# The last pair of a two-layer graph network: elu, residual sums and stores by quarters

## The chip, the cores and the metric

The kernel runs on one core of one Trainium2 chip. The metric is the device time of one execution in microseconds (us). A run's time is a little longer than the span of the profile, which goes from the first to the last instruction on the core.

## The reference, cut to what matters

The input x has 128 batches of 128 rows with 512 features, and adj is one 128 by 128 matrix a batch. Layer 0 is multi-head attention with eight heads, layer 1 a graph attention layer; both normalise their input first, and both are added to x. The change touches the end of layer 1, which is `h_prime`, `elu` and the last sum.

```python
# layer 0
h = maximum(layernorm(x), 0)
x = x + attention(h, adj, Wq, bq, Wk, bk, Wv, bv, Wo, bo)
# layer 1
h = maximum(layernorm(x), 0)
Wh = h @ W
e = leaky_relu(Wh @ a[:512] + transpose(Wh @ a[512:]), 0.2)
att = softmax(where(adj > 0.5, e, -9e15), axis=1)
h_prime = att @ Wh
x = x + elu(h_prime)          # elu(z) = z for z > 0, exp(z) - 1 otherwise
```

## The kernel before

The work goes by pairs of batches: p runs over 64 pairs. A pair's rows are held in `xs[p]`, a tile of 128 partitions (the rows of a batch) by 2 batches by 512 features in fp32. All of it is unrolled: each pair has a table of named steps (`steps`, L636 to L707), and three lists written out by hand say in which order the steps are issued, `HEAD` for the start, `ORDER` for the steady part, where steps of several pairs are interleaved, and `TAIL` for the last pairs (L569 to L606). In `TAIL`, `w4@-1` is step w4 of the last pair and `fb@-2` is step fb of the last but one. Each engine (PE for matmuls, ACT, DVE, POOL) and the SP queue, which issues the DMAs, takes its own instructions in this order; engines wait for each other with semaphores.

Layer 1 is computed as att @ h first and then times W. The product with W is done by a scheme with seven block products instead of eight (`PRODUCTS`, L124): the pair's two batches are the two row blocks t, and two halves of the features are the column blocks f. So the result z of a pair (a tile of 128 by 2 by 512) falls into four quarters (t, f) of 128 by 256, which `quarter(t, f)` selects. The steps w0, w1, w3, w2, w4, w5, w6 (`product_rows`, L282 to L292) are the seven products on TensorE, in that order. The steps zc0, zc2, zc4 and zc5 (`put1`, L463 to L467, on ACT) copy the first part of the quarters (0,0), (1,0), (1,1) and (0,1) out of PSUM, and wd1, wd4c and wd6 (`add1`, L469 to L471, on DVE) add a second part to the quarters (0,0), (1,1) and (1,0). So a quarter is complete at wd1 for (0,0), at wd4c for (1,1), at zc5 for (0,1) and at wd6 for (1,0), the last, which needs w6.

Then come four steps for the whole pair, with 1024 elements a partition each:

- ez (`elu`, L473 to L476): ez = exp(z), on ACT;
- fa (`finish_a`, L478 and L479): x = max(z, 0) + x, on DVE;
- fb (`finish_b`, L481 and L482): x = min(ez, 1) + x, on DVE. The -1 of elu is in a constant added earlier;
- so (`store`, L484 and L485): one DMA of 512 KB from the SP queue to `out`.

For every pair but the last these steps are interleaved with the work of later pairs. The list ends with the last pair's steps:

```
fb@-2 w2@-1 gs3@-1 zc2@-1 so@-2 w4@-1 zc4@-1 w5@-1 wd4c@-1 w6@-1 zc5@-1 wd6@-1 fa@-1 ez@-1 fb@-1 so@-1
```

Of the kernel before, what the change touches and what calls it, by code (L numbers as in the profile page):

```python
# [8 lines left out]
F32 = mybir.dt.float32  # L9
AF = mybir.ActivationFunctionType  # L10
OP = mybir.AluOpType
AX = mybir.AxisListType

P = 128
# [10 lines left out]
def kernel(  # L25
# [18 lines left out]
    nc = tc.nc  # L44
    B, S, E = x.shape
# [9 lines left out]
    work = ctx.enter_context(tc.tile_pool(name="work", bufs=1))  # L55
# [4 lines left out]
    xs, x0s, adjs, adjTs, hAs, hSs = {}, {}, {}, {}, {}, {}  # L60

    def both(src, p):
        return src[2 * p : 2 * p + 2].rearrange("b p f -> p b f")

    def load_x(p):

        xs[p] = io.tile([P, 2, E], F32, name="x")
        if p < 2:
            for i in range(2):
                nc.sync.dma_start(xs[p][:, i, :], x[2 * p + i])  # L70
        else:
            nc.sync.dma_start(xs[p], both(x, p))
# [96 lines left out]
    l1s, h1s, wts, pbs, pgs, gTs, zs, ezs, posts, hns, pts, onces = ({} for _ in range(12))  # L169
# [127 lines left out]
    def quarter(t, f):  # L297

        return slice(None), t, slice(f * 2 * P, (f + 1) * 2 * P)

    def scores(b):
        p, i = divmod(b, 2)
        g, h = divmod(p, 2)
        qT, kT = qks[g, "q"][h], qks[g, "k"][h]
        cols = slice(i * S, (i + 1) * S)

        sc = [ps1.tile([P, C, S], F32, name="sc", tag="ps1") for _ in range(2)]
        for j in range(C):
            for s in range(2):
                r = slice(s * D, (s + 1) * D)  # L310
                nc.tensor.matmul(sc[s][:, j, :], qT[r, j, cols], kT[r, j, cols], start=True, stop=True)  # L311
        scs[b] = sc
# [10 lines left out]
    def maxima(b):  # L323
        at, nmx, _, _ = ats[b]
        nc.vector.tensor_reduce(nmx, at, AX.X, OP.max, negate=True)  # L325
# [55 lines left out]
    def keep_context(b):  # L381
        nc.scalar.copy(rows_of(cxT, b % 2), pcs.pop(b))

    def output0(p, n):
        product_rows(p, cxT, wo_sb, "o", n)
# [84 lines left out]
        d = zs[p][quarter(t, f)]  # L470
        nc.vector.tensor_tensor(d, row_acc(p, "w", bank), d, OP.add)  # L471

    def elu(p):  # L473

        ezs[p] = work.tile([P, 2, E], F32, name="ez")
        nc.scalar.activation(ezs[p], zs[p], AF.Exp)  # L476

    def finish_a(p):  # L478
        nc.vector.scalar_tensor_tensor(xs[p], zs[p], 0.0, xs[p], op0=OP.max, op1=OP.add)  # L479

    def finish_b(p):  # L481
        nc.vector.scalar_tensor_tensor(xs[p], ezs.pop(p), 1.0, xs[p], op0=OP.min, op1=OP.add)  # L482

    def store(p):  # L484
        nc.sync.dma_start(both(out, p), xs.pop(p))  # L485
# [38 lines left out]
    N = B // 2  # L524
# [7 lines left out]
    def listed(text, mark):  # L532
# [69 lines left out]
        w5@-3 od6@-1 st1@-1 g0@-2 zc5@-3 st0@-1 g1@-2 ge0@-2 fa@-3 pw@-1 w0@-2 ge1@-2 ez@-3 gs2@-2 w1@-2 gs0@-2 gs1@-2  # L602
        w3@-2 nm@-1 zc0@-2 h20@-1 wd1@-2 w2@-2 h21@-1 d01@-1 d10@-1 zc2@-2 w4@-2 d00@-1 d11@-1 zc4@-2 pb@-1 wm@-1
        wd4c@-2 pr@-1 w6@-2 m1@-1 gs3@-2 e1@-1 w5@-2 sw@-1 fb@-3 zc5@-2 g0@-1 g1@-1 wd6@-2 ge0@-1 so@-3 fa@-2 w0@-1
        ge1@-1 ez@-2 gs2@-1 w1@-1 gs0@-1 gs1@-1 w3@-1 zc0@-1 wd1@-1 fb@-2 w2@-1 gs3@-1 zc2@-1 so@-2 w4@-1 zc4@-1 w5@-1
        wd4c@-1 w6@-1 zc5@-1 wd6@-1 fa@-1 ez@-1 fb@-1 so@-1  # L606
    """
    HEAD, ORDER, TAIL = listed(HEAD, "@"), listed(ORDER, ":"), listed(TAIL, "@")

    def start_steps(p):  # L610

        table = {}
        if 0 <= p < 4:
            table["pp"] = lambda: st0[p][2]()
            for i in range(2):
                table[f"hn{i}"] = lambda i=i: rows_hidden(p, i)
                table[f"tp{i}"] = lambda i=i: turn_hidden(p, i)
                table[f"ev{i}"] = lambda i=i: keep_hidden(p, i)
        if p == 0:
            weights = {"v": (wv_sb, wvT), "q": (wq_sb, wqT), "k": (wk_sb, wkT), "o": (wo_sb, woT), "w": (w1_sb, w1)}  # L620
            for n, (w, src) in weights.items():
                table["L" + n] = lambda w=w, src=src: nc.sync.dma_start(w[:, 0:4], src)
                for k in range(4):
                    table[f"W{n}{k}"] = lambda w=w, k=k: weight_sum(w, k)
            table |= {
                "Lc": lambda: load_row(c_sb, bo), "Lu0": lambda: load_row(us_sb, a1), "Lu1": lambda: load_row(ut_sb, a1, E),
                "ccp": product_c, "ccd": sum_c,
            }
            for i in range(2):
                table[f"sup{i}"] = lambda i=i: turn_u(i)  # L630
                table[f"sua{i}"] = lambda i=i: keep_u(i)
                for half in range(2):
                    table[f"cu{i}{half}"] = lambda i=i, half=half: dots_u(i, half)
        return table

    def steps(p):  # L636

        table = start_steps(p)
        for s, n in (("a", 2 * p), ("b", 2 * p + 1)):
            table |= {  # L640
                "sc" + s: lambda n=n: scores(n),
                "mx" + s: lambda n=n: maxima(n),
                "fl" + s: lambda n=n: flip_blocks(n),
                "bl" + s: lambda n=n: send_blocks(n),
                "pl" + s: lambda n=n: place_blocks(n),
                "pc" + s: lambda n=n: context(n),
                "pe" + s: lambda n=n: keep_context(n),
            }
            for k in range(4):
                table[f"ex{s}{k}"] = lambda n=n, k=k: exps(n, k)  # L650
                table[f"nm{s}{k}"] = lambda n=n, k=k: normalise(n, k)
            for k in range(2):
                table[f"at{s}{k}"] = lambda n=n, k=k: weigh(n, k)
                table[f"rc{s}{k}"] = lambda n=n, k=k: shares(n, k)
        for n in range(7):
            table[f"o{n}"] = lambda n=n: output0(p, n)
            table[f"w{n}"] = lambda n=n: output1(p, n)
        for k in range(4):
            table[f"cs{k}"] = lambda k=k: token_sum(cxT, cxT[:, 4:7], k)
            table[f"gs{k}"] = lambda k=k: token_sum(gTs[p], gTs[p][:, 4:7], k)  # L660
        for n, t, f in (("0", 0, 0), ("1", 0, 0), ("2", 1, 0), ("4", 1, 1), ("4c", 1, 1), ("5", 0, 1), ("6", 1, 0)):
            bank = "b" if n == "1" else "c" if n in ("4c", "6") else "a"
            table["od" + n] = lambda t=t, f=f, bank=bank: add0(p, t, f, bank)
            if bank == "a":
                table["zc" + n] = lambda t=t, f=f: put1(p, t, f)
            else:
                table["wd" + n] = lambda t=t, f=f, bank=bank: add1(p, t, f, bank)
        for i in range(2):
            table[f"st{i}"] = lambda i=i: stats1(p, i)
            table[f"h2{i}"] = lambda i=i: hidden1(p, i)  # L670
            table[f"g{i}"] = lambda i=i: gather1(p, i)
            table[f"ge{i}"] = lambda i=i: keep_gathered(p, i)
            for k in range(2):
                table[f"d{i}{k}"] = lambda i=i, k=k: dot1(p, i, k)
        table |= {
            "lt": lambda: load_adjT(p), "pw": lambda: l1s[p][2](), "nm": lambda: centre1(p), "pb": lambda: scores1(p), "wm": lambda: mask1(p),
            "pr": lambda: leaky1(p), "m1": lambda: maxima1(p), "e1": lambda: exps1(p), "sw": lambda: normalise1(p),
            "ez": lambda: elu(p), "fa": lambda: finish_a(p), "fb": lambda: finish_b(p), "so": lambda: store(p),
            "sh": lambda: shift(p),
        }  # L680
        table["lx"] = lambda: load_x(p)
        if p + 1 < N:
            table["la"] = lambda: load_adj(p + 1)
        if p + 4 < N:
            table |= {
                "f0": lambda: fetch0(p + 4), "lT": lambda: load_xT(p + 4),
                "hd0": lambda: hidden(p + 4, 0), "hd1": lambda: hidden(p + 4, 1),
            }
        if p + 5 < N:
            table |= {  # L690
                "l0": lambda: load_x0(p + 5), "t0": lambda: stats0(p + 5, 0), "t1": lambda: stats0(p + 5, 1),
                "s0": lambda: spread0(p + 5),
            }
        g, odd = divmod(p, 2)
        if odd and (g + 2) * 2 < N:
            for k in range(4):
                table[f"hs{k}"] = lambda k=k: hidden_sum(g + 2, k)
        if (g + 1) * 2 < N:
            for k, u in enumerate(SEQ[10:] if odd else SEQ[:10], 1):
                def unit(k=k, u=u):  # L700
                    posts[p, k] = product(g + 1, u[0], int(u[1]))
                table[f"U{k}"] = unit
                if int(u[1]) in FIRSTS:
                    table[f"F{k}"] = lambda k=k: posts[p, k][0]()
                if int(u[1]) in ADDS:
                    table[f"A{k}"] = lambda k=k: posts[p, k][1]()
        return table  # L707
# [59 lines left out]
```

## Time and profile before

| what | us |
|---|---|
| median of 4 runs | 2367.74 |
| lowest, highest | 2366.84, 2368.40 |
| the profiled execution's own time | 2368.2 |
| its span | 2366.4 |
| TensorE busy | 2340.9 |
| DVE busy | 2005.7 |
| ACT busy | 1437.9 |
| copy of one quarter, z<-row_a 128x256 (L467, ACT, mean) | 0.370 |
| add of one quarter, z<-row_c 128x256 (L471, DVE, mean) | 0.420 |
| exp of a pair, ez<-z 128x1024 (L476, ACT, mean) | 1.058 |
| x<-z,x 128x1024 (L479, DVE, mean) | 1.196 |
| x<-ez,x 128x1024 (L482, DVE, mean) | 1.218 |
| store out<-x of 512 KB (L485), issue to landing, smallest and median | 2.8, 6.0 |

Times of instructions are those of one profiled execution. They are given in microseconds from the start of the span. A busy time is the sum of what an engine's instructions took. In a group's line, the part behind "idle before" is the time in which the engine had nothing to run ahead of these instructions, and the name behind the arrow is what ended it. The DMA share is the mean busy share of the core's 16 DMA engines. The clock that TensorE was granted is 0.999 of full speed in this execution.

### The profile page before, as it was taken

How to read it: one execution, taken by the hardware profiler on the slowest of the kernel's cores; microseconds unless marked ns; L12 is line 12 of the kernel's file. 1: busy time of each engine (PE TensorE's matmuls, PEld its weight loads, DVE VectorE, ACT ScalarE, POOL GpSimd, SP SyncE). 2: the span in 40 equal slices, each digit the busy share in tenths (PEclk: the TensorE clock that was granted, in tenths of full speed). 3: DMA queues.
4: the chain of work that ended last, by engine and by line, in shares of the span. 5: the costliest groups of instructions: out<-in, count | busy, mean ns of one | idle time of the engine just before them, and what ended most of it. 6: DMA issues, size and time to landing. Idle time of an engine off the chain costs nothing.

```text
span 2366.4 us, 40912 instructions
## 1 busy us (share of the span) xinstructions
PE 2340.9 (99%) x14264; PEld 2060.5 (87%) x14264; DVE 2005.7 (85%) x4037; ACT 1437.9 (61%) x4811; POOL 221.8 (9%) x323
## 2 busy tenths in 40 slices
PE   7999999999999999999999999999999999999997
PEld 6888888888888888888888888888888888888886
DVE  7788888888888888888888888888888888888887
ACT  3656566665566665656665666556656566665674
POOL 1000100101101101011011010010110100101000
PEclk9999999999999999999999999999999999999999
DMA  5445545445544554445455444544554545544432
GB/s 174 123 118 126 132 122 138 134 127 129 138 127 134 131 134 123 127 133 138 125 134 129 139 126 125 138 130 125 134 141 128 131 120 140 130 130 119 123 112 87
DMA packets 255277, 306.11 MB, mean 129 GB/s; under 512 B 21856, under 2 KB 181600, under 8 KB 254432
## 3 DMA queue, kind: packets, MB, share of 16 engines
q1 hardware_dynamic: 251568, 303.37, 47.8%
q8 instruction: 113, 1.85, 0.4%
q14 instruction: 92, 0.75, 0.1%
q0 software_dynamic: 1920, 0.13, 0.1%
q10 hardware_dynamic: 1584, 0.01, 0.0%
HBM read 202.64 MB, written 100.79 MB: 128 GB/s over the span
## 4 chain that ended last, share of the span: by engine, by line
PE 97%; DVE 2%; DMA 1%; issue 0%; ACT 0%; POOL 0%; SPq 0%; DVEq 0%; ACTq 0%; POOLq 0%
PE acc_a L249 28%; PE row_a L290 23%; PE acc_c L249 14%; PE row_c L290 9%; PE acc_b L249 7%; PE sc L311 5%; PE pc L375 5%; PE pg L453 5%; PE pb L421 1%; DMA wq<-in_wqT 0%; DVE junk L412 0%; PE pt L188 0%; DVE st L159 0%; DMA x<-in_x 0%; DVE x L482 0%
## 5 line engine op out<-in xcount | busy, mean ns | idle before, releaser
L330 ACT ACTIVATE at<-at,nmx 128x128 f32<-128x128 f32 x1024 | 396.3, 392 | 12.1 <-DVE nmx L325 9.6
L467 ACT COPY z<-row_a 128x256 f32<-128x256 f32 x256 | 94.8, 370 | 431.2 <-PE row_a L290 307.5
L339 ACT ACTIVATE at<-at,rs 128x128 f32<-128x128 f32 x1024 | 323.6, 394 | 4.0 <-DVE rs L334 3.9
L290 PE MATMUL row_a<-w,gT 128*128 128x256 f32 x1280 | 319.5, 380 | 1.7 <-ACT z L467 1.4
L290 PE MATMUL row_a<-wo,cxT 128*128 128x256 f32 x1280 | 318.7, 380 | 0.3 <-DVE cxT L147 0.3
L290 PEld LDWEIGHTS row_a<-w,gT 128*128 128x128 f32 x1280 | 242.1, 190 | 37.1 <-ACT z L467 2.6
L290 PEld LDWEIGHTS row_a<-wo,cxT 128*128 128x128 f32 x1280 | 233.9, 190 | 27.9 <-DVE cxT L147 0.5
L163 POOL TENSOR_SCALAR mv<-mv 128x2 f32<-128x2 f32 x128 | 30.7, 240 | 2090.7 <-DVE mv L160 2056.4
L266 ACT ACTIVATE kT<-acc_a,bk 128x256 f32<-128x256 f32 x256 | 107.2, 471 | 164.5 <-PE acc_a L249 163.1
L266 ACT ACTIVATE qT<-acc_a,bq 128x256 f32<-128x256 f32 x256 | 106.4, 469 | 164.1 <-PE acc_a L249 164.1
L330 ACT ACTIVATION_READ_ACCUMULATOR at<-at,nmx 128x1 f32 x1024 | 195.0, 190 | 0.0
L159 DVE BATCH_NORM_STATS2 st<-x 128x6 f32<-128x512 f32 x256 | 174.5, 682 | 7.4 <-DMA x<-in_x 5.2
L389 DVE TENSOR_TENSOR x<-row_a,x 128x256 f32<-128x256 f32 x320 | 133.1, 416 | 47.8 <-PE row_a L290 39.3
L318 DVE SCALAR_TENSOR_TENSOR at<-sc,adj 128x512 f32<-128x512 f32 x256 | 169.7, 684 | 4.6 <-PE sc L311 2.0
L346 DVE STREAM_TRANSPOSE tr<-at 128x1024 f32<-128x1024 f32 x128 | 158.2, 1236 | 9.5 <-ACT at L339 8.7
L325 DVE TENSOR_REDUCE nmx<-at 128x8 f32<-128x1024 f32 x128 | 155.8, 1217 | 3.2
L164 POOL TENSOR_TENSOR mv<-mv,mhalf 128x2 f32<-128x2 f32 x128 | 144.5, 1129 | 10.7
L453 PEld LDWEIGHTS pg<-w,h 128*128 128x128 f32 x1024 | 133.5, 192 | 7.0 <-issue 0.7
L311 PEld LDWEIGHTS sc<-kT,qT 64*128 64x128 f32 x2048 | 119.7, 188 | 21.2 <-issue 20.2
L453 PE MATMUL pg<-w,h 128*128 128x128 f32 x1024 | 134.3, 275 | 0.1
L290 PE MATMUL row_c<-w,gT 128*128 128x256 f32 x512 | 131.6, 379 | 1.0 <-DVE z L471 1.0
L311 PE MATMUL sc<-kT,qT 64*128 64x128 f32 x2048 | 132.4, 279 | 0.0
(126 smaller groups left out, 4895.4 us busy)
## 6 DMA issues: line engine op xcount, KB each, us to landing
blocks<-tr SPq DMA_DIRECT2D x128, 512.0 KB, 2.9
aT<-blocks SPq DMA_DIRECT2D x512, 128.0 KB, 3.5
x<-in_x SPq DMA_DIRECT2D x123, 512.0 KB, 4.0
out<-x SPq DMA_DIRECT2D x64, 512.0 KB, 6.0
hA<-in_xT SPq DMA_DIRECT2D x120, 256.0 KB, 4.4
mr<-rows SPq DMA_DIRECT2D x60, 256.0 KB, 4.7
adj<-in_adj SPq DMA_DIRECT2D x64, 128.0 KB, 5.3
adjT<-in_adjT SPq DMA_DIRECT2D x64, 128.0 KB, 5.2
```

Source lines behind the costliest of these rows:

```text
L159: nc.vector.bn_stats(st, src[:, i, :])
L164: nc.gpsimd.tensor_tensor(mv[:, :, 1], mv[:, :, 1], mhalf.to_broadcast([P, 2]), OP.pow)
L249: nc.tensor.matmul(acc[:, m, :], lhsT, rhs, start=fresh and m == 0 and c == 0, stop=c == 1, skip_group_check=True)
L266: nc.scalar.activation(dst(t, f)[:, m, :], a[:, m, :], AF.Identity, bias=bias[:, j : j + 1])
L290: nc.tensor.matmul(acc, left[:, la, c, :], w[:, wb, c, :], start=n in (0, 3) and c == 0, stop=c == 1, skip_group_check=True)
L311: nc.tensor.matmul(sc[s][:, j, :], qT[r, j, cols], kT[r, j, cols], start=True, stop=True)
L318: nc.vector.scalar_tensor_tensor(ats[b][0][:, k * C : (k + 1) * C, :], scs[b][k], QSCALE, adjs[p][:, i : i + 1, :].to_broadcast([P, C, S]) ...
L325: nc.vector.tensor_reduce(nmx, at, AX.X, OP.max, negate=True)
L330: nc.scalar.activation(at[:, j, :], at[:, j, :], AF.Exp, bias=nmx[:, j : j + 1], accum_out=sums[:, j : j + 1])
L339: nc.scalar.activation(at[:, j, :], at[:, j, :], AF.Copy, scale=rs[:, j : j + 1])
L346: nc.vector.transpose(trs[b], at.rearrange("p h (j k) -> p j h k", k=Q))
L453: nc.tensor.matmul(pg[:, c, :], h1s[p][0][:, i, c * P : (c + 1) * P], wts[p][:, i, :], start=True, stop=True)
```

## The change

For the last pair alone, the steps ez, fa, fb and so are replaced. Each of elu, finish_a and finish_b now takes a part of the tiles, and is called once for each quarter (steps qe, qa, qb with the quarter's t and f behind), as soon as that quarter of z is complete. The store is cut in three: qs1 stores the second half of the features of batch t = 1, after the quarters (0,0) and (1,1); qs0 stores all of batch t = 0, after (0,1); qs2 stores the first half of the features of batch t = 1, after (1,0). All other pairs call the same functions for the whole tile. The steps of TensorE are the same and in the same order.

```diff
-    def elu(p):
-
-        ezs[p] = work.tile([P, 2, E], F32, name="ez")
-        nc.scalar.activation(ezs[p], zs[p], AF.Exp)
-
-    def finish_a(p):
-        nc.vector.scalar_tensor_tensor(xs[p], zs[p], 0.0, xs[p], op0=OP.max, op1=OP.add)
-
-    def finish_b(p):
-        nc.vector.scalar_tensor_tensor(xs[p], ezs.pop(p), 1.0, xs[p], op0=OP.min, op1=OP.add)
+    ALL = slice(None), slice(None), slice(None)
+
+    def elu(p, part=ALL):
+
+        if p not in ezs:
+            ezs[p] = work.tile([P, 2, E], F32, name="ez")
+        nc.scalar.activation(ezs[p][part], zs[p][part], AF.Exp)
+
+    def finish_a(p, part=ALL):
+        d = xs[p][part]
+        nc.vector.scalar_tensor_tensor(d, zs[p][part], 0.0, d, op0=OP.max, op1=OP.add)
+
+    def finish_b(p, part=ALL):
+        d = xs[p][part]
+        nc.vector.scalar_tensor_tensor(d, ezs[p][part], 1.0, d, op0=OP.min, op1=OP.add)
+
+    def store_rows(p, t, part):
+        nc.sync.dma_start(out[2 * p + t][:, part], xs[p][:, t, part])
...
-        ge1@-1 ez@-2 gs2@-1 w1@-1 gs0@-1 gs1@-1 w3@-1 zc0@-1 wd1@-1 fb@-2 w2@-1 gs3@-1 zc2@-1 so@-2 w4@-1 zc4@-1 w5@-1
-        wd4c@-1 w6@-1 zc5@-1 wd6@-1 fa@-1 ez@-1 fb@-1 so@-1
+        ge1@-1 ez@-2 gs2@-1 w1@-1 gs0@-1 gs1@-1 w3@-1 zc0@-1 wd1@-1 fb@-2 w2@-1 gs3@-1 zc2@-1 so@-2 w4@-1 qe00@-1
+        qa00@-1 qb00@-1 zc4@-1 w5@-1 wd4c@-1 qe11@-1 qa11@-1 qb11@-1 qs1@-1 w6@-1 zc5@-1 qe01@-1 qa01@-1 wd6@-1 qb01@-1
+        qs0@-1 qe10@-1 qa10@-1 qb10@-1 qs2@-1
...
+        if p == N - 1:
+            for step in ("ez", "fa", "fb", "so"):
+                table.pop(step)
+            for x, t, f in (("00", 0, 0), ("10", 1, 0), ("11", 1, 1), ("01", 0, 1)):
+                table["qe" + x] = lambda t=t, f=f: elu(p, quarter(t, f))
+                table["qa" + x] = lambda t=t, f=f: finish_a(p, quarter(t, f))
+                table["qb" + x] = lambda t=t, f=f: finish_b(p, quarter(t, f))
+            table |= {
+                "qs0": lambda: store_rows(p, 0, slice(0, E)),
+                "qs1": lambda: store_rows(p, 1, slice(E // 2, E)), "qs2": lambda: store_rows(p, 1, slice(0, E // 2)),
+            }
```

## The prediction

> **What bounds the kernel now.** I read the page's summary first, then its chain that ended last, then the instructions of the last 15 us in order of time, then the waits of the SP queue, and last the DMA traffic of the final 4 us in small stretches.
>
> ```profile
> span 2366.4 us, 40912 instructions
> ## 1 busy us (share of the span) xinstructions
> PE 2340.9 (99%) x14264; PEld 2060.5 (87%) x14264; DVE 2005.7 (85%) x4037; ACT 1437.9 (61%) x4811; POOL 221.8 (9%) x323
> ...
> ## 4 chain that ended last, share of the span: by engine, by line
> PE 97%; DVE 2%; DMA 1%; issue 0%; ACT 0%; POOL 0%; SPq 0%; DVEq 0%; ACTq 0%; POOLq 0%
> ```
>
> TensorE is busy 99% of the span and holds 97% of the chain. The change touches none of that: it concerns the last of 64 pairs, and on it only what comes after TensorE's last product. So the question is how long the kernel runs on once TensorE has stopped. The timeline of all engines over the last stretch (start, duration, engine, line, operation) gives it:
>
> ```profile
> start us, us, engine line op out<-in xcount [idle before <-releaser]
> ...
> 2358.00 1.03 PE L290 MATMUL row_c<-w,gT 128*128 128x256 f32 x4
> 2358.20 0.37 ACT L467 COPY z<-row_a 128x256 f32<-128x256 f32 x1 [1.22 <-PE row_a L290]
> 2359.06 0.42 DVE L471 TENSOR_TENSOR z<-row_c,z 128x256 f32<-128x256 f32 x1 [1.63 <-PE row_c L290]
> 2359.58 1.06 ACT L476 ACTIVATE ez<-z 128x1024 f32<-128x1024 f32 x1 [1.01 <-DVE z L471]
> 2359.59 1.23 DVE L479 SCALAR_TENSOR_TENSOR x<-z,x 128x1024 f32<-128x1024 f32 x1
> 2360.92 1.22 DVE L482 SCALAR_TENSOR_TENSOR x<-ez,x 128x1024 f32<-128x1024 f32 x1
> ```
>
> TensorE's last product, w6, ends at 2359.03. DVE adds it to z (2359.06 to 2359.48). Only then do elu (L476, ACT, 1.06 us) and finish_a (L479, DVE, 1.23 us) start, side by side, each over the whole pair, 1024 elements a partition; finish_b (L482) follows finish_a, not elu: elu was done at 2360.64, finish_a at 2360.82, and finish_b runs from 2360.92 to 2362.14. The SP queue issues the store of 512 KB at 2362.17 (L485's issues in the trace). What follows is seen in the SP queue's waits and in the traffic of the end (columns: stretch, its length, busy time of the engines, clock, DMA share, GB/s):
>
> ```profile
> engine line waited for: us in total, times, longest us
> ...
> SPq L763 <- DMA out<-x: 2.0, 1, 2.0
> ```
>
> ```profile
> core 0: us, PE busy (x) PEld busy (x) DVE busy (x) ACT busy (x) POOL busy (x), PEclk, DMA share, GB/s
> ...
> 2362.60:2363.00 0.40, 0.00 (x0) 0.00 (x0) 0.00 (x0) 0.00 (x0) 0.00 (x0) 1.00 0.00 0
> 2363.00:2363.50 0.50, 0.00 (x0) 0.00 (x0) 0.00 (x0) 0.00 (x0) 0.00 (x0) 0.57 0.84 332
> 2363.50:2364.00 0.50, 0.00 (x0) 0.00 (x0) 0.00 (x0) 0.00 (x0) 0.00 (x0) 0.50 0.97 385
> 2364.00:2364.60 0.60, 0.00 (x0) 0.00 (x0) 0.00 (x0) 0.00 (x0) 0.00 (x0) 0.50 0.72 277
> 2364.60:2366.40 1.80, 0.00 (x0) 0.00 (x0) 0.00 (x0) 0.00 (x0) 0.00 (x0) 0.50 0.00 0
> ```
>
> The store's first packets run from 2363.06, so 0.89 us after the issue; the data takes until 2364.4 to 2364.56 on the 16 engines; the trace's last landing event is at 2364.96. So 2.79 us go from issue to landing: 0.89 before the first packet, 1.35 of packets (16 packets of 2 KB an engine at 84 ns, the median of that size), 0.15 by which the engines end apart, 0.40 until the landing is seen. The stores of the two pairs before had 0.90 and 0.90 ahead of the data, and 0.39 and 0.40 behind it. After the landing come 1.47 us of final waits and barriers to the span's end at 2366.43. From TensorE's end to the span's end it is therefore 7.40 us = 0.03 + 0.42 + 2.66 (DVE's sums) + 0.03 + 2.79 (store) + 1.47. This 7.40 us, 0.31% of the span, is all that the change can act on, and 0.03 + 0.42 and most of 1.47 stay.
>
> **What the Trainium skill says.** "DMA: Bandwidth & Descriptors", section "Anatomy of one DMA — SWDGE (gpsimd) path", prices a DMA at a fixed part of about 2.0 us plus its bytes over 436 GB/s, and holds most of the fixed part to be the receipt of the write after the last byte. For 512 KB that is 3.2 us, against 2.79 here; the split differs too, with 0.89 us ahead of the data and 0.40 after it (the section is for the GpSimd path, these stores go from SP). The page "VectorE: DVE Perf Modes", section "The TRN2 errata — SBUF-src ops pay a fixed extra latency per instruction", says that each instruction pays a fixed extra, so that small pieces pay it per piece. The trace agrees: 1024 elements take 1.22 us (L482) and 256 take 0.42 us (L427, L471), so 1.04 ns an element and some 0.15 us fixed. "Perfetto Trace Analysis", section "Identifying Dependency Chains", says that an instruction that waits for several engines may have an EventSemaphore instruction put ahead of it. That is seen here: one stands before L479 and before L482, and they start 0.10 us after DVE's end, against 0.03 us where there is one wait (L447 after L446).
>
> **The change, part by part.** In the order of instructions of the changed program TensorE and POOL have the same lists; ACT, DVE and SP differ only in the last pair.
>
> *ACT.* One exp of 1024 becomes four of 256. No row shows 256: 0.42 us if 1.058 us is cut by 768 elements at 0.833 ns (the rate in "ScalarE: Activation LUTs", "Step-by-step: what each stage is for"), 0.49 if I go in a straight line from L330's 0.392 (128) to 1.058 (1024). I take 0.45 and keep both. The first stands behind the second z copy (ends 2355.38) and ends near 2355.9; queued behind it is the third copy, which isn't released before 2356.58 (TensorE), so 0.7 us of slack; TensorE's next product waits for that copy. The second exp starts when wd4c is done (2357.43) and ends near 2357.9; behind it the last copy, released at 2358.16, so 0.25 us of slack. The third follows that copy (2358.57), 2358.65 to 2359.1. The fourth starts at 2359.58, as L476 does now, and ends at 2360.03. No table load is added: the page's groups show one in the whole run, though Exp and Copy alternate at L476 and L467. Cost on the path: nothing; without this cover a longer exp would come 1:1 out of the slacks named.
>
> *DVE.* Two sums of 1024 become eight of 256 at 0.42 us, 0.34 us from start to start where independent (L471 to L482 at 2353.37 and 2353.71). The first two lie in DVE's idle time between 2355.26 and 2357.01; the sum wd4c, and behind it TensorE's w6, stand behind them. They need the first exp (2355.9) and end near 2356.4: 0.6 us of slack. The next two run from 2357.46 to 2358.4, in a gap that lasts to 2359.06. The fifth (qa01) is released by the last copy at 2358.6 and ends at 2359.03; wd6 stands behind it and starts at 2359.06 now. DVE can take a next instruction 0.34 us after the start before, at 2358.95: slack 0.1, so I cost it at nothing, and 0.1 if it fails. Then, after wd6 (2359.06 to 2359.48): qb01 at 2359.40, qa10 at 2359.74 to 2360.16, and qb10, which waits for two engines, 0.10 later: 2360.26 to 2360.68. So the sums end 2362.14 - 2360.68 = 1.46 us earlier. Its exp is done at 2360.03 and isn't the last to come: even 0.49 us changes nothing.
>
> *SP and DMA.* One store of 512 KB becomes 128, 256 and 128 KB, issued near 2358.45, 2359.87 and 2360.73, each issue 0.37 to 0.39 us, so the queue is free for each. Behind them on SP stand only the final waits; the first eight of them pass in 0.06 us each, done by 2361.7, before the landing. Each of the three waits for a landing long past on a counter of its own, none for the store before it. Data: the middle store has 8 packets an engine of 2 KB, from 2360.77 to 2361.6; the last starts at 2361.62 and has 8 packets of 1 KB at 46 ns (the trace's median of that size), 0.37 us. Issue to landing: 0.89 + 0.37 + 0.15 + 0.40 = 1.81 us, by the trace's parts; by the skill's formula 2.0 + 0.3 = 2.3. The range of the unknown is 1.8 to 2.8 (nothing of it shrinks); less than 1.8 is excluded as its fixed parts alone were the same in three stores. I take 1.81: 0.98 us saved, 0.5 or 0 at the other ends. The last store's counter is also the last one waited for, so that two of the final waits no longer stand behind the landing: 0.12 us.
>
> Sum, against the profiled execution: 1.46 + 0.98 + 0.12 = 2.56 us, so its span 2366.4 would be 2363.9. Its own time is 2368.2, 1.8 us around the span that stay; the median of the runs is 2367.74, and from it I predict 2367.74 - 2.5 = 2365.2.
>
> **The rivals.**
> (a) The store's time is fixed and doesn't shrink with its bytes. For it: the skill's 2 us. Against: 1.35 of 2.79 us are visible packets. Then 1.46 + 0.12 = 1.58 us: 2366.2.
> (b) The pieces don't come early: the smaller steps are held on ACT or DVE until wd6, and eight sums follow it. Against: the order of instructions has each wait on its own quarter's last writer. Eight sums from 2359.5 at 0.34 us end near 2362.3, 0.16 us later than now; the short store still gives 0.98 and 0.12: 0.94 us gained, 2366.8.
> (c) The slower side: the three stores complete one after the other on the SP queue's path, each beginning only as the one before has landed. From 2358.46, with the smallest landing seen of such a store, 2.8 us each: 2366.86 instead of 2364.96, and 0.12 less behind it, so +1.8 us: 2369.5. It decides against the change once a piece costs over (2365.08 - 2358.46) / 3 = 2.2 us. Against: four loads of L356 were issued 0.47 us apart and were in flight together.
> (d) Something outside the last 10 us moves, which nothing in the order of instructions suggests.
>
> **How the numbers follow.** The forecast has 0.82, (a) 0.09, (b) 0.04, (c) 0.02, (d) 0.03. The runs before lie from 2366.84 to 2368.4, 1.6 us apart, so two medians may stand off by 0.8 us. The forecast's low end, 2365.2 less 0.2 for its own roundings and 0.8 for the medians, is 2364.2; the high end takes in (a) with 0.8 us: 2367.0. Together these leave out less than 2 in 10. Of this kernel, a measurement can tell about 0.2%, 4.7 us, from no change. The forecast is 0.11%, and even sums that cost nothing would give no more than 2.66 + 0.98 + 0.12 = 3.8 us, 0.16%; so the forecast and (a) to (c) all lie within it; only (d) leaves it, 0.02 on the faster and 0.02 on the slower side.
>
> **What would show it.** In the profile after: TensorE's last product ends 7.4 - 2.5 = 4.9 us before the span's end; exps of 256 at 0.42 to 0.49 us; wd6 still within 0.1 us of w6's end; the last sum 1.2 us after wd6; three stores, the last landing 1.8 us after its issue. It would be wrong if that landing took 2.3 us or more, if TensorE waited for a copy behind an exp or for wd4c behind qb00, or if the spans differed elsewhere.

## The result, and the profile after

The changed kernel takes 2365.56 us (median of 41 runs, 2363.97 to 2367.72), beside 2368.2 us for the kernel before in the same comparisons (61 runs). The ratio is 0.9988, with a 95% interval from 0.9984 to 0.9992: 2.6 us, or 0.11%, less. The interval stays clear of 1. The forecast was 2365.2 in a range from 2364.2 to 2367.0.

The page of the changed kernel first. Nothing of TensorE's work has changed, and its share and the chain are what they were:

```profile
span 2364.5 us, 40926 instructions
## 1 busy us (share of the span) xinstructions
PE 2340.7 (99%) x14264; PEld 2060.4 (87%) x14264; DVE 2006.3 (85%) x4043; ACT 1438.5 (61%) x4814; POOL 221.8 (9%) x323
...
## 4 chain that ended last, share of the span: by engine, by line
PE 96%; DVE 2%; DMA 1%; issue 0%; ACT 0%; POOL 0%; SPq 0%; DVEq 0%; ACTq 0%; POOLq 0%
```

The question was how long the kernel runs on after TensorE's last product. Here is the same stretch of the timeline of all engines (start, duration, engine, line, operation, count):

```profile
start us, us, engine line op out<-in xcount [idle before <-releaser]
...
2358.74 1.03 PE L290 MATMUL row_c<-w,gT 128*128 128x256 f32 x4
...
2359.19 2.59 SPq L490 DMA_DIRECT2D out<-x  x3
...
2359.80 0.42 DVE L471 TENSOR_TENSOR z<-row_c,z 128x256 f32<-128x256 f32 x1
2360.14 0.41 DVE L487 SCALAR_TENSOR_TENSOR x<-ez,x 128x256 f32<-128x256 f32 x1
2360.26 0.42 ACT L479 ACTIVATE ez<-z 128x256 f32<-128x256 f32 x1 [0.50 <-DVE z L471]
2360.47 0.42 DVE L483 SCALAR_TENSOR_TENSOR x<-z,x 128x256 f32<-128x256 f32 x1
2361.00 0.43 DVE L487 SCALAR_TENSOR_TENSOR x<-ez,x 128x256 f32<-128x256 f32 x1
```

w6 ends at 2359.76. wd6 (L471) follows 0.04 us later as before, but now only three sums of 0.42 us come behind it: qb01, which belongs to the quarter (0,1), then qa10 and qb10 of the last quarter. The last exp (L479, 0.42 us) runs beside them and ends at 2360.68, ahead of qa10's end. The first of the three stores is issued at 2359.19, before w6 has ended. The SP queue's wait for stores has become 0.9 us in two pieces, from 2.0 us:

```profile
engine line waited for: us in total, times, longest us
...
SPq L783 <- DMA out<-x: 0.9, 2, 0.5
```

The traffic of the end (stretch, length, busy times, clock, DMA share, GB/s) shows why. The first store's data passes beside the sums, the second's from 2361.44, while the last is being issued, and only the last 128 KB follow:

```profile
core 0: us, PE busy (x) PEld busy (x) DVE busy (x) ACT busy (x) POOL busy (x), PEclk, DMA share, GB/s
2359.90:2360.40 0.50, 0.00 (x0) 0.00 (x0) 0.50 (x2) 0.14 (x1) 0.00 (x0) 1.00 0.63 227
2360.40:2361.40 1.00, 0.00 (x0) 0.00 (x0) 0.90 (x3) 0.28 (x1) 0.00 (x0) 1.00 0.06 17
2361.40:2362.30 0.90, 0.00 (x0) 0.00 (x0) 0.02 (x1) 0.00 (x0) 0.00 (x0) 1.00 0.76 291
2362.30:2362.90 0.60, 0.00 (x0) 0.00 (x0) 0.00 (x0) 0.00 (x0) 0.00 (x0) 1.00 0.62 219
2362.90:2364.60 1.70, 0.00 (x0) 0.00 (x0) 0.00 (x0) 0.00 (x0) 0.00 (x0) 0.52 0.00 0
```

From the trace's own times I take what I call the tail, from w6's end to the span's end: 7.41 us before, 4.75 now. Its parts, beside the prediction's terms:

| part of the tail | before | after | gained | predicted |
|---|---|---|---|---|
| w6's end to the end of the last sum | 3.12 | 1.66 | 1.46 | 1.46 |
| until the last store is issued | 0.03 | 0.03 | 0.00 | 0 |
| issue of the last store to its landing | 2.79 | 1.71 | 1.08 | 0.98 |
| landing to the span's end | 1.47 | 1.35 | 0.12 | 0.12 |
| sum | 7.41 | 4.75 | 2.66 | 2.56 |

The spans of the two profiled executions differ by less, 2366.43 - 2364.52 = 1.9 us, as w6 ended 0.74 us later in the second (2359.76, before 2359.02). That lies outside the tail: put side by side by number, TensorE's 14264 matmul records stand 0.84 us later from a quarter of the list to nearly its end. The shift comes in at 580 us, far ahead of the last pair; the section on why the prediction was right says what is found there.

### The profile page after: what moved, and what is told of

Its sections match the earlier page's. It is cut to its first block, busy times and chain, and to the rows that moved or that the text cites. A ratio compares the mean times of both kernels' runs of the same rounds, so it can differ in the third digit from the quotient of the medians.

```text
span 2364.5 us, 40926 instructions
## 1 busy us (share of the span) xinstructions
PE 2340.7 (99%) x14264; PEld 2060.4 (87%) x14264; DVE 2006.3 (85%) x4043; ACT 1438.5 (61%) x4814; POOL 221.8 (9%) x323
## 4 chain that ended last, share of the span: by engine, by line
PE 96%; DVE 2%; DMA 1%; issue 0%; ACT 0%; POOL 0%; SPq 0%; DVEq 0%; ACTq 0%; POOLq 0%
PE acc_a L249 28%; PE row_a L290 22%; PE acc_c L249 14%; PE row_c L290 9%; PE acc_b L249 7%; PE sc L311 5%; PE pc L375 5%; PE pg L453 5%; PE pb L421 1%; DMA aT<-blocks 0%; DMA wq<-in_wqT 0%; DVE junk L412 0%; DVE st L159 0%; PE pt L188 0%; DMA blocks<-tr 0%
```

## The experiments

All of them compute the whole result. I read the tail in each, since a single execution's span also carries what happened ahead of it.

**Sums by quarters, one store.** The edit undoes the store's part of the change alone:

```diff
-        qa00@-1 qb00@-1 zc4@-1 w5@-1 wd4c@-1 qe11@-1 qa11@-1 qb11@-1 qs1@-1 w6@-1 zc5@-1 qe01@-1 qa01@-1 wd6@-1 qb01@-1
-        qs0@-1 qe10@-1 qa10@-1 qb10@-1 qs2@-1
+        qa00@-1 qb00@-1 zc4@-1 w5@-1 wd4c@-1 qe11@-1 qa11@-1 qb11@-1 w6@-1 zc5@-1 qe01@-1 qa01@-1 wd6@-1 qb01@-1
+        qe10@-1 qa10@-1 qb10@-1 so@-1
...
-            for step in ("ez", "fa", "fb", "so"):
+            for step in ("ez", "fa", "fb"):
...
-            table |= {
-                "qs0": lambda: store_rows(p, 0, slice(0, E)),
-                "qs1": lambda: store_rows(p, 1, slice(E // 2, E)), "qs2": lambda: store_rows(p, 1, slice(0, E // 2)),
-            }
```

> The sums of the last pair go by quarters as in the changed kernel, but one store of 512 KB follows the last sum. I read the tail, from the end of TensorE's last product to the end of the span: 7.40 us in the kernel before, 4.75 in the changed one. Theory (three terms add up: earlier sums 1.46, shorter last store 1.08, two final waits 0.12): only the first stays, so a tail of 7.40 - 1.46 = 5.94 us, and a time 1.5 us under the kernel before. Rival (a store's time does not depend on its bytes, all of the gain is in the sums): a tail near 4.75. Rival (the gain is in the small stores alone): a tail near 7.4.

Measured: a tail of 5.95 us, and 2366.59 us beside 2368.36 (ratio 0.9991, interval 0.9982 to 1.0). The last sum ends 1.66 us after w6, as in the changed kernel; the store takes 2.79 us again, and the SP queue's wait is back at 2.0 us:

```profile
engine line waited for: us in total, times, longest us
...
SPq L779 <- DMA out<-x: 2.0, 1, 2.0
```

So 1.46 us come from the sums and 1.2 us from the stores, 1.08 of landing and 0.12 of final waits. This split rests on the tails; the interval of the times reaches to 1.0. The rival by which a store's time doesn't depend on its bytes is out, and so is the one that puts all of the gain in the small stores.

**Whole sums, three stores behind them.** The edit undoes the other part:

```diff
-        ge1@-1 ez@-2 gs2@-1 w1@-1 gs0@-1 gs1@-1 w3@-1 zc0@-1 wd1@-1 fb@-2 w2@-1 gs3@-1 zc2@-1 so@-2 w4@-1 qe00@-1
-        qa00@-1 qb00@-1 zc4@-1 w5@-1 wd4c@-1 qe11@-1 qa11@-1 qb11@-1 qs1@-1 w6@-1 zc5@-1 qe01@-1 qa01@-1 wd6@-1 qb01@-1
-        qs0@-1 qe10@-1 qa10@-1 qb10@-1 qs2@-1
+        ge1@-1 ez@-2 gs2@-1 w1@-1 gs0@-1 gs1@-1 w3@-1 zc0@-1 wd1@-1 fb@-2 w2@-1 gs3@-1 zc2@-1 so@-2 w4@-1 zc4@-1 w5@-1
+        wd4c@-1 w6@-1 zc5@-1 wd6@-1 fa@-1 ez@-1 fb@-1 qs1@-1 qs0@-1 qs2@-1
...
-            for step in ("ez", "fa", "fb", "so"):
-                table.pop(step)
...
+            table.pop("so")
```

> elu and the sums of the last pair stay whole, as in the kernel before; only the store is cut in three (128, 256, 128 KB), all three issued after the last sum. Theory (pieces overlap in flight, a piece costs its packets): the third is issued 0.79 us after the first, its data waits for the 256 KB ahead of it, so it lands 2.0 to 2.8 us after the first issue plus 0.0 to 0.1, and with 1.35 of final waits the tail is 7.0 to 7.35 us, near the kernel before. Rival (a store has a fixed 2.8 us): 3.14 + 0.79 + 2.79 + 1.35 = 8.1 us. Rival (stores complete one after the other): near 10 us, over 2 us slower than the kernel before.

Measured: a tail of 7.39 us, 2367.73 us beside 2368.36 (ratio 0.9997, interval 0.9989 to 1.0006). The three stores land 1.75, 2.12 and 2.02 us after their issues, and their issues are 0.40 and 0.48 us apart: they are in flight together, which rules out the slower rival (c) of the prediction. The traffic is one unbroken stretch, from 2363.47 to 2365.16:

```profile
core 0: us, PE busy (x) PEld busy (x) DVE busy (x) ACT busy (x) POOL busy (x), PEclk, DMA share, GB/s
2363.40:2363.90 0.50, 0.00 (x0) 0.00 (x0) 0.00 (x0) 0.00 (x0) 0.00 (x0) 0.50 0.74 254
2363.90:2364.60 0.70, 0.00 (x0) 0.00 (x0) 0.00 (x0) 0.00 (x0) 0.00 (x0) 0.50 0.92 354
2364.60:2365.20 0.60, 0.00 (x0) 0.00 (x0) 0.00 (x0) 0.00 (x0) 0.00 (x0) 0.50 0.71 249
2365.20:2366.90 1.70, 0.00 (x0) 0.00 (x0) 0.00 (x0) 0.00 (x0) 0.00 (x0) 0.50 0.00 0
```

The tail is 0.04 us over the upper end of what I expected, but that end was summed wrongly: its own terms give 3.14 + 2.8 + 0.1 + 1.35 = 7.39 us. Issued back to back, the second and the third issue take 0.42 and 0.45 us instead of the 0.35 and 0.33 of the changed kernel, so the third comes 0.88 us after the first and not 0.79. This doesn't set the end, as the third store's first packet, at 2364.63, comes 1.14 us after its issue, when the second store's data has passed. Beside the single store of the kernel before, the three take 1.69 us instead of 1.50 from the first packet to the last; lead and landing are 0.09 us shorter together, and the final waits 0.12. What follows: here, a store that is cut into pieces but starts only when all is done saves nothing. The pieces only help because the first two leave while DVE is still at work.

**The last store twice as large.**

```diff
-        qa00@-1 qb00@-1 zc4@-1 w5@-1 wd4c@-1 qe11@-1 qa11@-1 qb11@-1 qs1@-1 w6@-1 zc5@-1 qe01@-1 qa01@-1 wd6@-1 qb01@-1
+        qa00@-1 qb00@-1 zc4@-1 w5@-1 wd4c@-1 qe11@-1 qa11@-1 qb11@-1 w6@-1 zc5@-1 qe01@-1 qa01@-1 wd6@-1 qb01@-1
...
-                "qs0": lambda: store_rows(p, 0, slice(0, E)),
-                "qs1": lambda: store_rows(p, 1, slice(E // 2, E)), "qs2": lambda: store_rows(p, 1, slice(0, E // 2)),
+                "qs0": lambda: store_rows(p, 0, slice(0, E)), "qs2": lambda: store_rows(p, 1, slice(0, E)),
```

> As the changed kernel, but two stores of 256 KB, one for each batch of the pair, so that the last one has 256 KB instead of 128. Theory (a store's time grows with its packets: 8 of 2 KB an engine instead of 8 of 1 KB): issue to landing 2.04 us instead of 1.71, and a tail of 5.08 instead of 4.75 us. Rival (fixed time): 1.71 and 4.75.

Measured: issue to landing 2.04 us, a tail of 5.14 us (one execution of 2366.4 us, too few for a time). That is what the store of 256 KB took in the changed kernel; from the last store's 1.71 us by packets alone (8 of 84 ns instead of 8 of 46) it would be 2.01. The tail has 0.06 us more than expected, as the last store is now on the last counter but one, and one more of the final waits stands behind its landing (1.42 us from landing to end, against 1.35). Three sizes now give issue to landing 1.71, 2.04 and 2.79 us for 128, 256 and 512 KB, where an estimate by the formula of the Trainium skill ("DMA: Bandwidth & Descriptors", section "Anatomy of one DMA — SWDGE (gpsimd) path", so for the GpSimd path) gives 2.3, 2.6 and 3.2.

**One exp three times.** This takes away the cover under which I costed the exps at nothing:

```diff
-        qa00@-1 qb00@-1 zc4@-1 w5@-1 wd4c@-1 qe11@-1 qa11@-1 qb11@-1 qs1@-1 w6@-1 zc5@-1 qe01@-1 qa01@-1 wd6@-1 qb01@-1
+        qa00@-1 qb00@-1 zc4@-1 w5@-1 wd4c@-1 qe11@-1 qe11b@-1 qe11c@-1 qa11@-1 qb11@-1 qs1@-1 w6@-1 zc5@-1 qe01@-1 qa01@-1 wd6@-1 qb01@-1
...
+                if x == "11":
+                    table["qe11b"] = table["qe11c"] = table["qe11"]
```

> As the changed kernel, but the exp of the quarter (1,1) is done three times over, with the same output, so that ACT is held 0.8 to 0.9 us longer ahead of its last copy zc5. Theory (the exps cost nothing only because they end before the next copy is released, 0.25 us of slack there, and the sum wd6 stands behind qa01, which needs that copy): zc5 starts 0.6 us later, qa01 and wd6 0.5 to 0.6 us later, and the tail is 5.3 us. Rival (ACT is off the path in the tail, the exps are free whatever they take): 4.75 us.

Measured: a tail of 5.18 us, 0.42 more than in the changed kernel (one execution of 2364.39 us, whose w6 ended at 2357.44, the earliest of all). ACT's row and DVE's row in the trace of that kernel:

```profile
start us, us, engine line op out<-in xcount [idle before <-releaser]
2355.88 1.31 ACT L479 ACTIVATE ez<-z 128x256 f32<-128x256 f32 x3 [0.49 <-DVE z L471]
2357.10 0.35 ACT L467 COPY z<-row_a 128x256 f32<-128x256 f32 x1
```

```profile
start us, us, engine line op out<-in xcount [idle before <-releaser]
...
2357.23 0.43 DVE L487 SCALAR_TENSOR_TENSOR x<-ez,x 128x256 f32<-128x256 f32 x1 [0.92 <-ACT ez L479]
2357.57 0.42 DVE L483 SCALAR_TENSOR_TENSOR x<-z,x 128x256 f32<-128x256 f32 x1
2357.91 0.42 DVE L471 TENSOR_TENSOR z<-row_c,z 128x256 f32<-128x256 f32 x1
```

The three exps hold ACT until 2357.20; the copy zc5 behind them starts 0.34 us before w6's end instead of 0.83, and wd6 0.47 us after it instead of 0.04. So the exps cost nothing only as long as they end early enough, and the rival by which ACT doesn't matter in the tail is out. The way by which they cost is not the one that I expected: the copy is done at 2357.46, but qb11 has waited 0.92 us for the third exp, qa01 comes 0.34 us behind qb11, at 2357.57, and wd6 0.34 us behind qa01. By way of the copy alone wd6 would start near 2357.83 (an estimate: qa01 0.03 us after the copy, wd6 0.34 us later), 0.35 us late and not 0.43. The size was less than expected, 0.42 us instead of some 0.55: the slack ahead of the copy was 0.31 us (exp done 1.14 us and copy released 0.83 us ahead of w6's end), not 0.25, and qa01 and wd6 stand 0.34 us apart when both are ready, 0.46 in the changed kernel.

**The changed kernel again.** No edit.

> The changed kernel once more, for its tail and its time beside the next one. Theory (the tail is fixed by the order of the instructions, and what differs from run to run lies ahead of it): a tail within 0.05 of 4.75 us whatever the end of TensorE's last product is, and a time 2.6 us under the kernel before. Rival (part of the 2.6 us is chance): the tail moves by some tenths with the run.

Measured: a tail of 4.75 us, 2365.34 us beside 2367.55 (ratio 0.999, interval 0.9982 to 0.9998). w6 ended at 2358.67, 1.1 us earlier than in the first profile of the same program; each instruction in the tail stands within 0.01 us of where it stood from w6's end. Over all eight profiles of this study w6's end lies between 2357.44 and 2359.76 and doesn't order by kernel.

**Without the last add.** The experiments left DVE as the chain after w6: wd6, qb01, qa10, qb10. This version takes wd6 out of it. The steps zx11 and wx11 build the quarter (1,1), wz10 is the product with the identity, and `elu_psum` and `finish_a_psum` are `elu` and `finish_a` with row_a or row_c in the place of z:

```diff
-        ge1@-1 ez@-2 gs2@-1 w1@-1 gs0@-1 gs1@-1 w3@-1 zc0@-1 wd1@-1 fb@-2 w2@-1 gs3@-1 zc2@-1 so@-2 w4@-1 qe00@-1
-        qa00@-1 qb00@-1 zc4@-1 w5@-1 wd4c@-1 qe11@-1 qa11@-1 qb11@-1 qs1@-1 w6@-1 zc5@-1 qe01@-1 qa01@-1 wd6@-1 qb01@-1
+        ge1@-1 ez@-2 gs2@-1 w1@-1 gs0@-1 gs1@-1 w3@-1 zc0@-1 wd1@-1 zx11@-1 fb@-2 w2@-1 gs3@-1 zc2@-1 so@-2 w4@-1 wz10@-1 qe00@-1
+        qa00@-1 qb00@-1 wx11@-1 w5@-1 qe11@-1 qa11@-1 qb11@-1 qs1@-1 w6@-1 qe01@-1 qa01@-1 qb01@-1
...
+    def put_c(p, t, f):
+        nc.scalar.copy(zs[p][quarter(t, f)], row_acc(p, "w", "c"))
+
+    def add_by_product(p, t, f):
+        nc.tensor.matmul(
+            row_acc(p, "w", "c"), ident, zs[p][quarter(t, f)], start=False, stop=True, skip_group_check=True
+        )
...
+            for x, t, f, bank in (("01", 0, 1, "a"), ("10", 1, 0, "c")):
+                table["qe" + x] = lambda t=t, f=f, bank=bank: elu_psum(p, quarter(t, f), bank)
+                table["qa" + x] = lambda t=t, f=f, bank=bank: finish_a_psum(p, quarter(t, f), bank)
+            table["wx11"] = lambda: add1(p, 1, 1, "a")
+            table["zx11"] = lambda: put_c(p, 1, 1)
+            table["wz10"] = lambda: add_by_product(p, 1, 0)
```

> The changed kernel with the add wd6 taken out of the tail. The half sum z of the quarter (1,0) is added to the PSUM tile row_c by a product with the identity, in the gap in which TensorE waits ahead of w5; the quarter (1,1) is copied from row_c first and gets its other part from row_a on DVE; the exp and the first sum of the quarters (0,1) and (1,0) read PSUM, one after the other[...]. Theory (after w6 DVE is the chain: wd6, qb01, qa10, qb10, four sums of 256): with wd6 gone, exp 0.04 to 0.46, qa10 to 0.92 and qb10 to 1.38 us after w6's end instead of 1.66, so a tail of 4.47 us and 0.3 us less than the changed kernel. Rival (the store's landing sets the tail, not the sums): 4.75 us. Rival (the added product doesn't fit the gap of 0.46 us): w5 and w6 end up to 0.4 us later, which the tail doesn't show but the gap ahead of w5 does.

Measured: a tail of 4.44 us, 2364.79 us beside 2367.55 (ratio 0.9989, interval 0.9983 to 0.9996); beside it the changed kernel had 2365.34. The two intervals overlap, so that it beats the changed kernel is shown by the tail, 0.31 us shorter, and not by the times. Its end:

```profile
start us, us, engine line op out<-in xcount [idle before <-releaser]
...
2357.38 1.03 PE L290 MATMUL row_c<-w,gT 128*128 128x256 f32 x4
...
2358.45 0.38 ACT L490 ACTIVATE ez<-row_c 128x256 f32<-128x256 f32 x1 [0.48 <-PE row_c L290]
2358.46 0.42 DVE L487 SCALAR_TENSOR_TENSOR x<-ez,x 128x256 f32<-128x256 f32 x1
2358.86 0.42 DVE L494 SCALAR_TENSOR_TENSOR x<-row_c,x 128x256 f32<-128x256 f32 x1
2359.32 0.42 DVE L487 SCALAR_TENSOR_TENSOR x<-ez,x 128x256 f32<-128x256 f32 x1
```

The exp of the last quarter (L490) starts 0.04 us after w6; beside it DVE does the leftover sum of the quarter (0,1), then the last two. They end 1.34 us after w6 instead of 1.66, 0.04 us earlier than expected, as the exp takes 0.38 us here and not 0.42. So the steps behind w6, and not the landing alone, set the tail. The product with the identity, 0.59 us in the timeline's record, lies wholly in the gap ahead of w5: it ends at 2356.33, and w5 starts at 2356.42. Still 0.06 us are lost there: against w6's end, the copy zc2 stands at -4.07 instead of -4.01. The trace shows w5 waiting for the add wx11 (0.42 us on DVE), where it waited for the copy zc4 (0.37 us on ACT) before. That 0.06 us has to be taken off the gain, which leaves 0.26 us.

## Why the prediction was right

- **What bounds.** Right: the change acts on the tail alone, and its 7.4 us were the whole of what could be gained. TensorE's busy time is 2340.7 us, from 2340.9.
- **ACT.** Right, and shown in both directions: the exps of 256 take 0.42 us (I took 0.45, between 0.42 and 0.49) and cost nothing, and where the cover is taken away they do cost, though by way of qb11 on DVE and not of the copy alone. The slack behind the second exp was 0.31 us, not 0.25.
- **DVE.** Right to 0.01 us: qb01, qa10 and qb10 start 0.38, 0.71 and 1.23 us after w6's end, where the prediction's times give 0.37, 0.71 and 1.23. I had counted on wd6 not being held by qa01. It started 0.46 us after qa01 and 0.04 us after w6's end, as before, so TensorE released it and the cost was nothing. The experiment without the last add shows that this chain of sums sets when the last store goes.
- **SP and DMA.** Right in mechanism; the landing was the term whose size was most off, 1.71 instead of 1.81 us. That is also below the 1.8 us under which I had excluded it, as lead and landing had been the same in three stores; those three were all of 512 KB in 2 KB rows. By the packets' times, the lead ahead of the first was 0.85 us instead of 0.89, and the landing came 0.34 us after the last instead of 0.40; the packets took what they were costed at. The price by the section of the Trainium skill named above ("DMA: Bandwidth & Descriptors"), an estimate of 2.3 us, would have left only half of this gain.
- **The final waits.** Right: with the last store on the last counter, 0.12 us less stand behind the landing. The experiment with two stores gave half of it back. One detail was wrong and cost nothing: the eighth wait did not pass at once but stood 0.4 us for the second store's landing, ahead of the last one's.
- **The rivals.** (a) is out by the three sizes of store, (b) by the first profile after, where the steps of the first three quarters lie ahead of w6's end but for one sum, (c) by the three stores in flight together. (d) remains as what moves w6's end from execution to execution, by up to 2.3 us in the eight profiles. That it adds nothing between the kernels is shown only as closely as the medians tell: they lie 1.8, 0.6, 2.2 and 2.8 us under the kernel before where the tails are 1.5, 0.0, 2.7 and 3.0 us shorter (one store, whole sums, the changed kernel again, no last add).

The sum was 2.56 us against 2.66 in the tail and 2.6 by the medians. The time itself was 0.36 us over the forecast, as the kernel before had 2368.2 us in 61 runs and 2367.74 in the four that I started from. I had also held that under 0.2% nothing can be told from no change; with 41 and 61 runs, 0.11% could.

Where most of these 2.3 us come in can be read from the matmul records. One place is the start: eight products of 128x256 (L249) that begin at 15 us take 3.55 us in the profile of the kernel before, 3.48 and 3.13 in the two of the changed kernel and 2.11 in that with one exp three times; the slow ones take 0.63 us each, the others 0.38. The other is at 580 us: in the first profile of the changed kernel TensorE waits 0.91 us for a load (aT<-blocks, L356) and all that follows stands 1.1 us later; in its second profile and in that of the kernel before it doesn't wait there. Both places differ between two executions of one program. What stays open is why the first products are slow for longer, and why that load is late, in one execution and not in another; I made no experiment on it.

## What to carry to other kernels

When one engine is busy to within a per cent, look at what runs after it has stopped: here 7.4 us of 2366, a chain of whole-tile steps most of which could have been done for three quarters of their data beforehand. Cost such a tail from its end: here, a store cut in pieces gained only through what left before the last piece was ready, the last piece had best be small (1.71 us from issue to landing against 2.04 for twice the bytes), and even then 1.2 us of the store's lead and landing and 1.35 us of final waits stay. For an effect of 0.1%, read the tail in the trace, where it repeats to 0.01 us, and not the span, which moved by 2 us between executions.

## What was not expected of the hardware

- Between two executions of one program, the end of TensorE's last product moved by 1.1 us, yet everything after it repeated to 0.01 us.
- An exp of 128x256 takes 0.383 us when it reads PSUM (without the last add) and 0.416 us when it reads SBUF (the changed kernel).
- Stores issued one right after the other on the SP queue (whole sums, three stores) took 0.42 and 0.45 us to issue, against 0.33 to 0.35 for the same stores when they are apart. What makes the difference isn't shown.
